# A two-layer graph-attention kernel: VectorE's second inputs moved to PSUM, the last denominators summed on TensorE, LayerNorms in the value bank, the mask built in pieces

## The chip, the cores and the metric

The kernel runs on one core of one Trainium2 chip. The metric is the time of one execution on the device in microseconds (us). The engines are called by the names that the profile uses: PE is TensorE, PEld its weight loads, DVE is VectorE, ACT is ScalarE, POOL is GpSimd and SP is SyncE, which issues most transfers.

## The reference, cut to what matters

```python
def _gat_layer(h, mask, b):                       # N = 2048 nodes, D = 64
    scores = jnp.einsum('...nd,...md->...nm', h, h)
    scores = jnp.where(mask, scores, -1e16)
    attn = jax.nn.softmax(scores, axis=-1)
    return jnp.einsum('...nm,...md->...nd', attn, h) + b

mask = graph + eye(N) > 0
h    = einsum('bnc,hdc->bhnd', x, Wh)             # B = 8 batches, H = 4 heads
cat  = _gat_layer(h, mask, bh) -> [B, N, H*D]     # first layer
h2   = einsum('bnk,dk->bnd', leaky_relu(cat, 0.2), Wo)
z2   = leaky_relu(_gat_layer(h2, mask, bo), 0.2)  # second layer
out  = layernorm(z2) * gamma + beta
return layernorm(x + out)
```

Everything is fp32. The score matrices dominate: 2048 x 2048 for each of 32 pairs of batch and head, and for 8 batches in the second layer.

## The kernel before

The work is cut into 20 units. A unit is two heads (first layer, 16 units) or two batches (second layer, 4 units), stacked as 2 x 64 rows. A unit has four chunks of 512 query columns, a chunk has four periods, and a period has four blocks of 128 keys. In a period TensorE computes the scores of four blocks and then the values of the four blocks before them:

```python
def scores(self, c, m):
    ps = spsum(...)                        # 3 PSUM tiles of two banks
    for j in range(2):
        nc.tensor.matmul(ps[:, j*W:(j+1)*W], self.hT[rows, m*P:(m+1)*P], self.hT[rows, c*W:(c+1)*W], ...)
    e = slot([P, 2, W], F32, ...)
    nc.vector.tensor_tensor(e, ps, mask[c][:, m, :], OP.subtract)      # L523
    nc.scalar.activation(e, e, AF.Exp, bias=shift, scale=1.0)          # L525
    return e

def values(self, c, m, e):                 # O[c] is one PSUM bank, one buffer
    for j in range(2):
        nc.tensor.matmul(self.O[c][j*D:(j+1)*D, :], self.hN[:, m, j*D:(j+1)*D], e[:, j, :], ...)
```

The softmax denominators are sums of `e` over all 16 blocks and 128 partitions. GpSimd adds 12 of the 16 tiles (11 additions), VectorE the fourth tile of each period (L549, L553) and the two partial sums (L560); TensorE sums the result over the partitions with a matrix of ones. The rest is spread over the following periods, one step in each:

```python
def finish0(self, c):                      # one period after the last values
    nc.scalar.copy(self.osb[c], self.O[c])
    nc.vector.tensor_tensor(self.acc[c], self.acc[c], self.accd[c][0], OP.add)     # L560
def finish1(self, c):
    for j in range(2):
        nc.tensor.matmul(pz[j*D:(j+1)*D, :], ones, self.acc[c][:, j, :], ...)      # 64-column tiles
    nc.scalar.copy(zsb, pz)
    ... two small transfers spread one row of zsb over the partitions: zt
def finish2(self, c):
    nc.vector.reciprocal(rt, self.zt)
    nc.vector.tensor_tensor(stat[:, 0, :], stat[:, 0, :], self.zt, OP.add)         # L579
    nc.vector.tensor_tensor(stat[:, 1, :], stat[:, 1, :], rt, OP.add)
    ... rt to DRAM (rd) and back, broadcast over 64 partitions: rz
def finish3(self, c):
    nc.vector.tensor_tensor(z, z, self.rz[c], OP.mult)                             # L589
    nc.vector.scalar_tensor_tensor(z, z, SLOPE, z, OP.mult, OP.max)                # L590
def finish4(self, c): ...   # projection by Wo (first layer); turn and first LayerNorm (second)
def finish5(self, c): ...   # gamma, beta, + x, second LayerNorm, store (second layer)
```

Both LayerNorms work on a tile `y` in SBUF. `at(t, job)` puts a job behind the scores, values and additions of period `t`. The mask is built during the first unit from rows of the adjacency matrix, half a row block at a time.

Of the kernel before, what the change touches and what calls it, by code (L numbers as in the profile page):

```python
# [33 lines left out]
EPS = 1e-5  # L35
# [317 lines left out]
def fast_kernel(ctx: ExitStack, tc: tile.TileContext, x, adj, Wh, bh, Wo, bo, gamma, beta, out, flag):  # L353
# [11 lines left out]
    K = 2 * CB  # L365

    const = ctx.enter_context(tc.tile_pool(name="const", bufs=1))
    big = ctx.enter_context(tc.tile_pool(name="big", bufs=2))
    epool = ctx.enter_context(tc.tile_pool(name="epool", bufs=12))
    accs = ctx.enter_context(tc.tile_pool(name="accs", bufs=2))  # L370
    work = ctx.enter_context(tc.tile_pool(name="work", bufs=6))
# [11 lines left out]
    def tpsum(name):  # L383
        return psum.tile([P, W], F32, tag="t", name=name, bufs=1)
# [9 lines left out]
    ones = const.tile([P, D], F32, name="ones")  # L394
    nc.gpsimd.memset(ones, 1.0)
    shifts = const.tile([P, 3], F32, name="shifts")
    nc.gpsimd.memset(shifts[:, 0:1], -SHIFT1)
    nc.gpsimd.memset(shifts[:, 1:2], -SHIFT2)
    nc.gpsimd.memset(shifts[:, 2:3], BIG)
    mhalf = const.tile([P, K], F32, name="mhalf")  # L400
# [7 lines left out]
    stat = const.tile([P, 2, 8], F32, name="stat")  # L408
    nc.gpsimd.memset(stat, 0.0)
# [37 lines left out]
    def load_adj(r, h):  # L447
        st = slot([P, N // 2], I32, f"adj{r}_{h}")
        nc.sync.dma_start(out=st, in_=adj[r * P:(r + 1) * P, h * N // 2:(h + 1) * N // 2])
        return st  # L450

    def build_mask(r, h, st):
        if r // (NB // 2) == h:
            c0 = r * P - h * N // 2
            nc.vector.tensor_tensor(st[:, c0:c0 + P], st[:, c0:c0 + P], ident, OP.add)
        m = slot([P, N // 2], BF16, f"mrow{r}_{h}")
        if h == 0:
            nc.scalar.activation(m, st, AF.Relu, bias=shifts[:, 2:3], scale=-BIG)
        else:
            nc.vector.tensor_scalar(m, st, 0.0, BIG, OP.is_le, OP.mult)  # L460
        p = spsum(f"pm{r}_{h}", BF16)
        for k in range(NB // 2):
            nc.tensor.transpose(p[:, k * P:(k + 1) * P], m[:, k * P:(k + 1) * P], identb)  # L463
        c, i0 = divmod(r * P, W)
        dst = mask[c][:, h * NB // 2:(h + 1) * NB // 2, i0:i0 + P]
        src = p[:, :NB // 2 * P].rearrange("p (m i) -> p m i", i=P)
        if h == 0:
            nc.vector.tensor_copy(dst, src)
        else:
            nc.scalar.copy(dst, src)  # L470

    pw = tpsum("pw")
# [8 lines left out]
    class Unit:  # L481


        def __init__(self, n, bp, b2, hp):
            self.n, self.bp, self.b2, self.hp = n, bp, b2, hp
            self.second = hp is None
            self.osb, self.rz, self.acc, self.accd, self.O = {}, {}, {}, {}, {}
# [40 lines left out]
        def values(self, c, m, e):  # L528
            if m == 0:
                self.O[c] = psum.tile([P, W], F32, tag="o", name=f"o{self.n}_{c}", bufs=1)  # L530
            for j in range(2):
                nc.tensor.matmul(self.O[c][j * D:(j + 1) * D, :], self.hN[:, m, j * D:(j + 1) * D], e[:, j, :],  # L532
                                 start=(m == 0), stop=(m == NB - 1))

        def add_up(self, c, es):

            first = c not in self.acc
            if first:
                self.acc[c] = accs.tile([P, 2, W], F32, tag="acc", name=f"acc{self.n}_{c}")
                self.accd[c] = [es[3]]  # L540
                nc.gpsimd.tensor_tensor(self.acc[c], es[0], es[1], OP.add)  # L541
                nc.gpsimd.tensor_tensor(self.acc[c], self.acc[c], es[2], OP.add)  # L542
                return
            for e in es[:3]:
                nc.gpsimd.tensor_tensor(self.acc[c], self.acc[c], e, OP.add)  # L545
            if len(self.accd[c]) == 1:
                held = self.accd[c][0]
                t = accs.tile([P, 2, W], F32, tag="accd", name=f"accd{self.n}_{c}", bufs=1)
                nc.vector.tensor_tensor(t, held, es[3], OP.add)  # L549
                self.accd[c] = [t, 2]  # L550
            else:
                t = self.accd[c][0]
                nc.vector.tensor_tensor(t, t, es[3], OP.add)  # L553
                self.accd[c][1] += 1


        def finish0(self, c):
            self.osb[c] = wtile(f"osb{self.n}_{c}")
            nc.scalar.copy(self.osb[c], self.O[c])
            nc.vector.tensor_tensor(self.acc[c], self.acc[c], self.accd[c][0], OP.add)  # L560

        def finish1(self, c):
            n = self.n
            pz = tpsum(f"pz{n}_{c}")
            for j in range(2):
                nc.tensor.matmul(pz[j * D:(j + 1) * D, :], ones, self.acc[c][:, j, :], start=True, stop=True)  # L566
            zsb = wtile(f"zsb{n}_{c}")
            nc.scalar.copy(zsb, pz)
            self.zt = small.tile([P, 8], F32, tag="zt", name=f"zt{n}_{c}")
            with nc.allow_non_contiguous_dma(reason="2 KB"):  # L570
                for j in range(2):
                    nc.sync.dma_start(out=self.zt[j * D:(j + 1) * D, :],
                                      in_=zsb[j * D:j * D + 1, :].rearrange("o (p k) -> o p k", k=8))

        def finish2(self, c):
            n = self.n
            rt = small.tile([P, 8], F32, tag="rt", name=f"rt{n}_{c}")
            nc.vector.reciprocal(rt, self.zt)
            nc.vector.tensor_tensor(stat[:, 0, :], stat[:, 0, :], self.zt, OP.add)  # L579
            nc.vector.tensor_tensor(stat[:, 1, :], stat[:, 1, :], rt, OP.add)  # L580
            rd = dram.tile([2, W], F32, tag="rd", name=f"rd{n}_{c}")
            nc.sync.dma_start(out=rd.rearrange("j (p k) -> (j p) k", k=8), in_=rt)
            self.rz[c] = wtile(f"rz{n}_{c}")
            for j in range(2):
                nc.sync.dma_start(out=self.rz[c][j * D:(j + 1) * D, :], in_=rd[j].partition_broadcast(D))

        def finish3(self, c):
            z = self.osb[c]
            nc.vector.tensor_tensor(z, z, self.rz[c], OP.mult)  # L589
            nc.vector.scalar_tensor_tensor(z, z, SLOPE, z, OP.mult, OP.max)  # L590

        def finish4(self, c):
            n, z = self.n, self.osb[c]
            p = tpsum(f"pp{n}_{c}")
# [11 lines left out]
            for i in range(CB):  # L606
                nc.tensor.transpose(p[:, i * P:(i + 1) * P], z[:, i * P:(i + 1) * P], ident)
            rows = p.rearrange("p (k d) -> p k d", d=D)
            self.y = wtile(f"y{n}_{c}")
            self.norm(c, rows, 0)  # L610

        def finish5(self, c):
            if not self.second:
                return
            y = self.y.rearrange("p (k d) -> p k d", d=D)
            nc.vector.tensor_mul(y, y, gam.unsqueeze(1).to_broadcast([P, K, D]))
            nc.vector.tensor_add(y, y, bet.unsqueeze(1).to_broadcast([P, K, D]))
# [5 lines left out]
            nc.vector.tensor_add(self.y, self.y, xr)  # L623
            self.norm(c, y, 1)
            yv = self.y.rearrange("p (i b d) -> p i b d", b=2, d=D)
# [3 lines left out]

        def norm(self, c, src, tag):  # L630
            n = self.n
            y = self.y.rearrange("p (k d) -> p k d", d=D)
            st = small.tile([P, 4, K], F32, tag="st", name=f"st{n}_{c}_{tag}")
            sq = wtile(f"sq{n}_{c}_{tag}").rearrange("p (k d) -> p k d", d=D)
            nc.vector.tensor_reduce(st[:, 0, :], src, AX.X, OP.add)
            nc.vector.tensor_scalar(st[:, 0, :], st[:, 0, :], 1.0 / D, None, OP.mult)
            nc.vector.tensor_tensor(y, src, st[:, 0, :].unsqueeze(2).to_broadcast([P, K, D]), OP.subtract)  # L637
            nc.scalar.square(sq, y)  # L638
            nc.vector.tensor_reduce(st[:, 1, :], sq, AX.X, OP.add)
            nc.vector.tensor_scalar(st[:, 2, :], st[:, 1, :], 1.0 / D, EPS, OP.mult, OP.add)  # L640
            nc.gpsimd.tensor_tensor(st[:, 3, :], st[:, 2, :], mhalf, OP.pow)  # L641
            nc.vector.tensor_mul(y, y, st[:, 3, :].unsqueeze(2).to_broadcast([P, K, D]))  # L642
# [21 lines left out]
    transpose_x(0, x0, 0)  # L664
    transpose_x(0, x0, 1)
    raw = {}
    halves = [(r, h) for r in range(NB) for h in range(2)]
    AHEAD = 3
    for k in range(2 * CB):
        raw[k] = load_adj(*halves[k])  # L670
        if k >= AHEAD:
            build_mask(*halves[k - AHEAD], raw.pop(k - AHEAD))
    for part in range(4):
        units[0].prepare(part)
    for k in range(2 * CB, len(halves) + AHEAD):
        t = (k - 2 * CB) // 2

        def job(k=k):
            if k < len(halves):
                raw[k] = load_adj(*halves[k])  # L680
            build_mask(*halves[k - AHEAD], raw.pop(k - AHEAD))
# [97 lines left out]
```

## Time and profile before

The time is 3559.51 us (median of three runs, 3554.14 to 3559.91).

| | before |
|---|---|
| granted TensorE clock, mean | 0.910 |
| busy: TensorE, VectorE, ScalarE, GpSimd | 81%, 83%, 47%, 67% |
| one TensorE period, undisturbed | 7.22 us |
| a first-layer unit (four chunks) after the first | 153 to 159 us; 168 just after a second-layer unit |
| a second-layer unit | 212 to 216 us |
| first scores; end of the first unit's first chunk | 46.8 us; 119.9 us |

A unit's length is read between the first finishing operations of successive units (the accumulation L560 before, the maximum L583 after). In a line of groups the columns are: line, engine, operation, output and inputs by the program's names, shapes, count, then busy us in total and mean ns of one, then the engine's idle time just ahead of them and what ended it. In a timeline they are start, length in us, engine, line, operation, count, and in brackets the idle time before it with its releaser. Four undisturbed periods and the small TensorE work of a chunk would make about 32 us, so a first-layer chunk (38 to 40 us) loses 6 to 8 us and a second-layer chunk (54 us) over 20.

### The profile page before, as it was taken

How to read it: one execution, taken by the hardware profiler on the slowest of the kernel's cores; microseconds unless marked ns; L12 is line 12 of the kernel's file. 1: busy time of each engine (PE TensorE's matmuls, PEld its weight loads, DVE VectorE, ACT ScalarE, POOL GpSimd, SP SyncE). 2: the span in 40 equal slices, each digit the busy share in tenths (PEclk: the TensorE clock that was granted, in tenths of full speed). 3: DMA queues.
4: the chain of work that ended last, by engine and by line, in shares of the span. 5: the costliest groups of instructions: out<-in, count | busy, mean ns of one | idle time of the engine just before them, and what ended most of it. 6: DMA issues, size and time to landing. Idle time of an engine off the chain costs nothing.

```text
span 3551.6 us, 31313 instructions
## 1 busy us (share of the span) xinstructions
PE 2870.1 (81%) x11526; PEld 986.6 (28%) x11526; DVE 2963.9 (83%) x2368; ACT 1654.9 (47%) x1577; POOL 2363.0 (67%) x929
## 2 busy tenths in 40 slices
PE   5668888988876788898887688888889888877663
PEld 3232323332222232232222222323323232222221
DVE  4668888889888888888888888898888889888886
ACT  3435555554543445555444345555545555443332
POOL 2437777777755677777775577777777777766553
PEclk8779999999988899999998899999999999988886
DMA  3210000000000000000000000000000000000000
GB/s 118 63 33 7 10 7 7 19 10 7 7 16 13 12 10 7 19 7 10 7 10 18 10 10 10 6 19 6 10 7 7 7 10 6 7 10 18 12 15 22
DMA packets 93125, 53.57 MB, mean 15 GB/s; under 512 B 78466, under 2 KB 78530, under 8 KB 92962
## 3 DMA queue, kind: packets, MB, share of 16 engines
q1 hardware_dynamic: 92162, 51.02, 5.1%
q8 instruction: 92, 1.51, 0.2%
q0 software_dynamic: 176, 0.26, 0.1%
q14 instruction: 71, 0.58, 0.1%
q10 hardware_dynamic: 624, 0.20, 0.0%
HBM read 46.60 MB, written 4.52 MB: 14 GB/s over the span
## 4 chain that ended last, share of the span: by engine, by line
PE 38%; DVE 29%; issue 19%; POOL 8%; DMA 4%; ACT 2%; SPq 0%; DVEq 0%; POOLq 0%; ACTq 0%
PE o L532 17%; PE s L520 15%; DVE e L523 11%; POOL acc L545 5%; DVE osb L589 5%; DVE accd L553 4%; DMA rz<-rd 4%; DVE acc L560 3%; PE ph L501 2%; PE pz L566 2%; POOL acc L542 1%; DVE y L642 1%; POOL acc L541 1%; ACT e L525 1%; PE pp L599 1%
## 5 line engine op out<-in xcount | busy, mean ns | idle before, releaser
L545 POOL TENSOR_TENSOR acc<-acc,e 128x1024 f32<-128x1024 f32 x720 | 1869.8, 2597 | 467.2 <-ACT e L525 421.1
L525 ACT ACTIVATE e<-e,shifts 128x1024 f32<-128x1024 f32 x1280 | 1451.0, 1149 | 1355.6 <-DVE e L523 1348.3
L523 DVE TENSOR_TENSOR e<-s,mask 128x1024 f32<-128x1024 f32 x1280 | 1477.6, 1212 | 278.5 <-PE s L520 266.6
L520 PE MATMUL s<-hT 64*128 64x512 f32 x4096 | 1096.5, 646 | 340.5 <-DVE e L523 284.5
L532 PE MATMUL o<-e,hN 128*64 128x512 f32 x5120 | 1285.2, 648 | 0.0
L520 PEld LDWEIGHTS s<-hT 64*128 64x128 f32 x4096 | 393.1, 195 | 944.8 <-DVE e L523 459.4
L532 PEld LDWEIGHTS o<-e,hN 128*64 128x64 f32 x5120 | 367.1, 149 | 933.8 <-issue 712.5
L520 PE MATMUL s<-h2T 64*128 64x512 f32 x1024 | 286.8, 679 | 196.1 <-DVE e L523 166.1
L541 POOL TENSOR_TENSOR acc<-e,e 128x1024 f32<-128x1024 f32 x80 | 188.9, 2362 | 345.6 <-ACT e L525 345.6
L553 DVE TENSOR_TENSOR accd<-accd,e 128x1024 f32<-128x1024 f32 x160 | 310.4, 1940 | 0.0
L641 POOL TENSOR_TENSOR st<-st,mhalf 128x8 f32<-128x8 f32 x32 | 52.7, 1647 | 358.9 <-DVE st L640 358.9
L542 POOL TENSOR_TENSOR acc<-acc,e 128x1024 f32<-128x1024 f32 x80 | 248.6, 3107 | 6.3
L589 DVE TENSOR_TENSOR osb<-osb,rz 128x512 f32<-128x512 f32 x80 | 220.1, 2751 | 4.9 <-DMA rz<-rd 4.9
L590 DVE SCALAR_TENSOR_TENSOR osb<-osb 128x512 f32<-128x512 f32 x80 | 210.8, 2635 | 2.8
L520 PEld LDWEIGHTS s<-h2T 64*128 64x128 f32 x1024 | 97.4, 200 | 350.9 <-DVE e L523 215.7
L560 DVE TENSOR_TENSOR acc<-acc,accd 128x1024 f32<-128x1024 f32 x80 | 169.4, 2118 | 2.8
L579 DVE TENSOR_TENSOR stat<-stat,zt 128x8 f32<-128x8 f32 x80 | 169.3, 2116 | 0.0
L642 DVE TENSOR_TENSOR y<-y,st 128x512 f32<-128x512 f32 x32 | 81.8, 2555 | 56.3 <-POOL st L641 56.3
L549 DVE TENSOR_TENSOR accd<-e,e 128x1024 f32<-128x1024 f32 x80 | 121.1, 1514 | 0.0
L463 PE MATMUL pm<-identb,mrow 128*128 128x128 bf16 x256 | 29.5, 286 | 87.0 <-DVE mrow L460 49.1
L566 PE MATMUL pz<-acc,ones 128*64 128x512 f32 x320 | 85.0, 611 | 9.5 <-DVE acc L560 9.5
L638 ACT ACTIVATE sq<-y 128x512 f32<-128x512 f32 x32 | 20.1, 629 | 142.8 <-DVE y L637 142.8
(70 smaller groups left out, 811.1 us busy)
## 6 DMA issues: line engine op xcount, KB each, us to landing
rz<-rd SPq DMA_DIRECT2D x160, 128.0 KB, 2.8
adj<-in_adj_dram SPq DMA_DIRECT2D x32, 512.0 KB, 3.7
x<-in_x_dram SPq DMA_DIRECT2D x16, 256.0 KB, 3.7
xr<-in_x_dram SPq DMA_DIRECT2D x32, 128.0 KB, 2.6
out_dram<-y SPq DMA_DIRECT2D x32, 128.0 KB, 2.0
zt<-zsb SPq DMA_DIRECT2D x160, 2.0 KB, 1.7
rd<-rt SPq DMA_DIRECT2D x80, 4.0 KB, 1.4
ws<-in_L_gnn_Wh_dram ACTq DMA_DIRECT2D x2, 64.0 KB, 4.7
```

The costliest lines, as they stand in the source:

```text
L520: nc.tensor.matmul(ps[:, j * W:(j + 1) * W], self.hT[rows, m * P:(m + 1) * P], self.hT[rows, c * W:(c + 1) * W], start=True, stop=True)
L523: nc.vector.tensor_tensor(e, ps.rearrange("p (j i) -> p j i", j=2), mask[c][:, m, :].unsqueeze(1).to_broadcast([P, 2, W]), OP.subtract)
L525: nc.scalar.activation(e, e, AF.Exp, bias=shifts[:, 1:2] if self.second else shifts[:, 0:1], scale=1.0)
L532: nc.tensor.matmul(self.O[c][j * D:(j + 1) * D, :], self.hN[:, m, j * D:(j + 1) * D], e[:, j, :], start=(m == 0), stop=(m == NB - 1))
L541: nc.gpsimd.tensor_tensor(self.acc[c], es[0], es[1], OP.add)
L542: nc.gpsimd.tensor_tensor(self.acc[c], self.acc[c], es[2], OP.add)
L545: nc.gpsimd.tensor_tensor(self.acc[c], self.acc[c], e, OP.add)
L553: nc.vector.tensor_tensor(t, t, es[3], OP.add)
L560: nc.vector.tensor_tensor(self.acc[c], self.acc[c], self.accd[c][0], OP.add)
L579: nc.vector.tensor_tensor(stat[:, 0, :], stat[:, 0, :], self.zt, OP.add)
L589: nc.vector.tensor_tensor(z, z, self.rz[c], OP.mult)
L590: nc.vector.scalar_tensor_tensor(z, z, SLOPE, z, OP.mult, OP.max)
```

## The change

Its intent is to take VectorE off the critical path. Where VectorE had two inputs in SBUF, one is now in PSUM. The last three blocks' denominators, which come too late for GpSimd, go straight to TensorE in 32-column tiles. The LayerNorms stay in the PSUM bank of the values, and the matrix that turns the tile also takes out the mean. The mask comes in pieces that each finish two key blocks of one query chunk. The core of the diff:

```diff
+    DIRECT = 3
-    epool = ... bufs=12        # slots for e
+    epool = ... bufs=14
+    def opsum(name):           # two value banks instead of one and one "t" bank
+        return psum.tile([P, W], F32, tag="o", name=name, bufs=2)
...
-        def add_up(self, c, es): ... three tiles to GpSimd, the fourth to VectorE
+        def add_up(self, c, m, e):
+            elif m < NB - DIRECT:
+                nc.gpsimd.tensor_tensor(acc, acc, e, OP.add)
+            else:
+                self.terms[c].append(e)
...
+        def sums(self, c):
+            for k in range(half):
+                for s in range(2):
+                    for j in range(2):
+                        q = (2 * s + j) * 32
+                        nc.tensor.matmul(pz[q:q + 32, :W], ones, terms[s * half + k][:, j, :],
+                                         start=(k == 0), stop=(k == half - 1), tile_position=(0, q))
+            nc.scalar.copy(zsb, pz[:, :W])
+            ... four small transfers instead of two: zt
+            nc.scalar.mul(o5, self.O[c], SLOPE)
+            nc.vector.tensor_tensor(self.O[c], self.O[c], o5, OP.max)
+        def invert(self, c):
+            nc.vector.tensor_reduce(zall[:, k, :], zt, AX.X, OP.add)
+            nc.vector.reciprocal(rt, zall[:, k, :])
+            ... rt to DRAM and back
+        def scale(self, c):
+            nc.vector.tensor_tensor(self.z[c], self.O[c], self.z[c], OP.mult)
...
-                nc.tensor.transpose(p[:, i * P:(i + 1) * P], z[:, i * P:(i + 1) * P], ident)
+                nc.tensor.matmul(p[:, i * P:(i + 1) * P], z[:, i * P:(i + 1) * P], centre, ...)
+        def norm1(self, c, y):  # y is the PSUM bank
+            nc.vector.tensor_mul(y, y, self.rstd(c, y, 0))   # square, reduce, ScalarE, power on GpSimd
+            nc.vector.tensor_mul(y, y, gam...)
+            nc.vector.tensor_add(y, y, bet...)
+            nc.vector.tensor_add(y, y, xr)
+        def norm2(self, c): ... mean, power, product, store
...
+                at((t + 1, "mid"), lambda u=u, c=c: u.sums(c))      # between scores and values
+                at(t + 1, lambda u=u, c=c: u.invert(c))             # after the values
+                at(t + 2, lambda u=u, c=c: u.scale(c))
+                at(t + 3, lambda u=u, c=c: u.project(c))            # holds norm1
+                at(t + 4, lambda u=u, c=c: u.norm2(c))
```

## The prediction

> **What bounds the kernel now.** I read the page first (busy shares, chain, groups), then the timeline of single chunks, then durations of single lines, then the table by stage.
>
> ```profile
> PE 2870.1 (81%) x11526; PEld 986.6 (28%) x11526; DVE 2963.9 (83%) x2368; ACT 1654.9 (47%) x1577; POOL 2363.0 (67%) x929
> PE 38%; DVE 29%; issue 19%; POOL 8%; DMA 4%; ACT 2%; SPq 0%; DVEq 0%; POOLq 0%; ACTq 0%
> L545 POOL TENSOR_TENSOR acc<-acc,e 128x1024 f32<-128x1024 f32 x720 | 1869.8, 2597 | 467.2 <-ACT e L525 421.1
> L523 DVE TENSOR_TENSOR e<-s,mask 128x1024 f32<-128x1024 f32 x1280 | 1477.6, 1212 | 278.5 <-PE s L520 266.6
> L553 DVE TENSOR_TENSOR accd<-accd,e 128x1024 f32<-128x1024 f32 x160 | 310.4, 1940 | 0.0
> L589 DVE TENSOR_TENSOR osb<-osb,rz 128x512 f32<-128x512 f32 x80 | 220.1, 2751 | 4.9 <-DMA rz<-rd 4.9
> L590 DVE SCALAR_TENSOR_TENSOR osb<-osb 128x512 f32<-128x512 f32 x80 | 210.8, 2635 | 2.8
> L560 DVE TENSOR_TENSOR acc<-acc,accd 128x1024 f32<-128x1024 f32 x80 | 169.4, 2118 | 2.8
> L579 DVE TENSOR_TENSOR stat<-stat,zt 128x8 f32<-128x8 f32 x80 | 169.3, 2116 | 0.0
> ```
>
> No engine is full; the chain alternates between TensorE and VectorE. A 128x8 addition (L579) takes 2116 ns: that is waiting, not work. The durations (minimum/median/maximum) of two lines say how much:
>
> ```profile
> L590 DVE SCALAR_TENSOR_TENSOR osb<-osb x80: 691/2711/2717, 173.6 to 3526.7; 128x512 f32<-128x512 f32 x80
> L545 POOL TENSOR_TENSOR acc<-acc,e x720: 2337/2381/3249, 62.0 to 3498.9; 128x1024 f32<-128x1024 f32 x180
> ```
>
> 691 ns is the operation, the other 2.0 us most of a GpSimd addition. The timeline shows one undisturbed period (four blocks of scores, four of values) of a first-layer unit, then the place in a second-layer unit where VectorE is late:
>
> ```profile
> 626.80 3.70 PE L520 MATMUL s<-hT 64*128 64x512 f32 x16
> 630.43 3.65 PE L532 MATMUL o<-e,hN 128*64 128x512 f32 x16
> 634.02 2.85 PE L520 MATMUL s<-hT 64*128 64x512 f32 x12
> ...
> 1124.69 2.82 DVE L642 TENSOR_TENSOR y<-y,st 128x512 f32<-128x512 f32 x1 [1.76 <-POOL st L641]
> 1127.43 3.35 DVE L560 TENSOR_TENSOR acc<-acc,accd 128x1024 f32<-128x1024 f32 x1
> 1131.98 2.08 PE L520 MATMUL s<-hT 64*128 64x512 f32 x4 [9.58 <-DVE e L523]
> 1133.99 5.61 PE L532 MATMUL o<-e,hN 128*64 128x512 f32 x16
> ```
>
> The period has a TensorE pitch of 634.02 - 626.80 = 7.22 us. TensorE runs only three score tiles ahead of VectorE, so every lump of VectorE work beyond some 2.6 us stops it: here 9.58 us, after which the same matmuls ran slower (2.08 us for 4, elsewhere 1.13). By stage (length, busy times, granted clock): start and mask, a first-layer unit, a second-layer unit with its neighbours.
>
> ```profile
> 0.00:300.00 300.00, 200.52 (x854) 88.07 (x856) 181.51 (x152) 119.95 (x113) 118.03 (x61) 0.83 0.20 64
> 592.00:749.00 157.00, 139.35 (x580) 48.48 (x576) 137.87 (x105) 82.38 (x79) 115.55 (x44) 0.96 0.06 14
> 1870.00:2083.00 213.00, 155.76 (x566) 50.99 (x562) 177.62 (x157) 81.72 (x80) 126.85 (x51) 0.84 0.06 14
> ```
>
> Spacing the values' matmuls through the trace, a first-layer chunk (four periods) takes 8.2 + 11.8 + 10.1 + 8.1 = 38.2 us, 39.3 with the preparation (157 / 4); a second-layer chunk 12.3 + 20.6 + 13.5 + 8.1 = 54.5 us. There are 64 and 16 of them.
>
> **What the Trainium skill says.** "SBUF — State Buffer", Who interferes with whom: VectorE with two SBUF inputs contends with a GpSimd instruction that reads SBUF, with at most one it does not. The trace agrees (691 against 2711 ns above; L523, one input from PSUM, stays at 1212). "VectorE: DVE Perf Modes", The perf-mode tier table: fp32 tensor_tensor runs at the base rate from SBUF and PSUM alike, so the move costs no rate; the trace has 686 ns for h2T<-h2T,pp (512 columns, one input from PSUM). "TensorEngine Tiling (Array Packing)", Tiling Modes: with 128 rows, 32-column tiles give four tiles at once, and changing the mode drains the array. The trace shows only two at once: 16 value records of 512 columns in some 3.6 us. "TensorE: Matmul & The Clock Gate", Part 1: an idle array has its clock lowered; the 0.84 of the second-layer stage against 0.96 agrees.
>
> **The change part by part.** Durations of rows not shown (L549, L580, the LayerNorm lines, ph, pn) are from the same view of groups.
> VectorE loses L553 310, L549 121, L560 169, L589 220, L590 211, L579 and L580 182: 1213 us. It gains, per chunk, a maximum in PSUM and a scaling at 0.69 each and a reduction of some 0.17: 80 x 1.55 = 124. LayerNorms: nine operations of 0.69 on 16 chunks, about 100 instead of some 165; mask: 32 copies of 0.69 = 22 instead of 62. Estimated VectorE busy time: 2964 - 1213 + 124 - 65 - 40 = 1770 us, 22 us of a chunk. It stops being a bound.
> GpSimd gets 12 additions per chunk instead of 11, at the undisturbed 2.4 us: 960 x 2.4 = 2304, + 53 for the powers = 2360 us, 29.5 us a chunk, below TensorE.
> ScalarE: the slope copy replaces the eviction of O; unchanged, 1660 us.
> TensorE: the denominators become eight matmuls of 512 columns in groups of four at once, two rounds of 0.86 + about 0.2 for switching = 1.9 us instead of 1.0. TensorE per first-layer chunk: 4 x 7.22 = 28.9, + 1.9, + projection 1.0, + preparation 1.5 (the next unit's projection ph, 32 x 1.7, its transposes pn, 40 x 1.05, and those of x, over 80 chunks) = 33.3 us.
> A wait takes its place. The denominators' inversion now stands in the same period as their sum; VectorE waits in order for their transfer. From the period's start: last exponential at 6.9, zsb copied at 7.5, four issues of 0.55, landing 1.7 to 1.85: 11.1 us; with reduction, reciprocal and the next e, 12.7. TensorE starts the next period at 3.6 + 1.9 + 3.6 = 9.1 and wants that tile at 9.1 + 2.6 = 11.7. About 1.1 us lost per chunk: 34.4 us. The rd/rz round trip (5.1 us at the end of the trace) ends at 16.6, just before the next period needs VectorE.
> Second layer: norm1 starts after the projection (8.2 us), then square 0.65, reduction 0.7, ScalarE 0.3, GpSimd 1.65, four times 0.7: VectorE free at 14.6, the next e at 15.8, wanted at 10.8: 5.0 lost. norm2 has the same loop but starts before the period ends: 3.4 lost. Inversion 1.5. Sum 28.9 + 1.9 + 1.0 + 9.9 = 41.7; the slower clock after such gaps cost up to 2.9 us before (5.61 - 3.65 + 2.08 - 1.13), I take 3.3 for both: 45 us.
> Start: the first scores needed eight mask halves and came at 46.8 us; now they need two turned pieces, about 28. The mask then takes 15 periods of 9.1 instead of some 15 to 17, plus waits of ScalarE on GpSimd for the diagonal of perhaps 12 us: first unit 4 x 34.4 + 15 x 1.85 + 12 = 178 us. The end, after the last values, was 54 us; its links now add to about 42.
> Sum: 28 + 178 + 60 x 34.4 + 16 x 45 + 42 = 28 + 178 + 2064 + 720 + 42 = 3032. Against 3559 the gains are 60 x 4.9 = 294, 16 x 9.5 = 152, and about 80 at start and end.
>
> **The rivals.**
> TensorE bound without the new waits: 28.9 + 1.9 + 1.0 + 1.5 on all chunks and no LayerNorm stall, about 2750 us. For it: the 1.00 clock of the quoted period. Against: VectorE is in order, and the LayerNorm loops over ScalarE and GpSimd remain.
> The new wait is bigger: if the four small transfers or rz come 2 us later than I count, each chunk loses 2 to 4 us, 160 to 320: 3200 to 3350. For it: SyncE issues in order, with the mask's loads in the same queue. Against: zt lands in 1.7 us throughout.
> GpSimd becomes the bound: 29.5 us of 34.4, and it lags by up to some 7 us within a chunk; with 14 slots a score tile may wait for its slot, or a power queue behind additions. Worth perhaps 60 to 100 us. Against: nothing contends any more, and on average it catches up.
> The four-tile matmuls run two at a time: + 1.7 x 80 = 137 us. Nothing in this trace decides it.
>
> **Range and chances.** The TensorE part (about 2670 us of the sum) is measured here; the waits, some 300 us, are argued. A miss of a third of them is 100 us each way. Predicted 3030 us, range 2920 to 3140. Faster by over 2% 0.97, within 2% 0.02, slower 0.01: only a wrong sign of several terms could eat 500 us.
>
> **What would show it right or wrong.** Right: no VectorE group with median above 1.3 us; GpSimd additions at about 2.4 us, 960 of them; VectorE about 50 to 60% busy, TensorE above 88%; first-layer chunks of 33 to 36 us; the reduction of zt waiting for its transfer; second-layer chunks of 42 to 48 with a wait on GpSimd's power. Wrong: the pz group at 3 us or more a chunk, TensorE's waits on e longer than 1.5 us in first-layer chunks, e or exponentials waiting for GpSimd, or a granted clock below 0.9 in the first layer.

## The result, and the profile after

The kernel after takes 2929.29 us (median of four runs, 2927.95 to 2929.53); the kernel before took 3557.11 us in the same rounds. Ratios here are the mean time of one kernel's runs over that of the other's of the same rounds, so they are not quite the ratio of the medians quoted. This one is 0.8234, with a 95% interval from 0.822 to 0.8249. The granted clock rose from 0.910 to 0.977. The predicted 3030 us were 101 us too high, and the range holds the result near its lower end.

The page of the kernel after, its busy line, its chain and three of its groups:

```profile
PE 2730.6 (93%) x12550; PEld 967.9 (33%) x12550; DVE 1799.2 (61%) x1861; ACT 1656.4 (57%) x1625; POOL 2331.8 (80%) x1025
PE 60%; ACT 14%; DVE 11%; DMA 5%; issue 4%; SPq 3%; POOL 2%; ACTq 0%; DVEq 0%; POOLq 0%
L554 POOL TENSOR_TENSOR acc<-acc,e 128x1024 f32<-128x1024 f32 x880 | 2079.9, 2363 | 79.5 <-ACT e L534 13.0
L583 DVE TENSOR_TENSOR o<-o,o 128x512 f32<-128x512 f32 x80 | 56.0, 700 | 175.8 <-ACT o L582 175.8
L599 DVE TENSOR_TENSOR z<-o,z 128x512 f32<-128x512 f32 x80 | 55.2, 690 | 53.5 <-DMA z<-rd 53.4
```

VectorE lost 1165 us of busy time and has fallen behind TensorE and GpSimd. Its share of the chain fell from 29% to 11%, TensorE's rose from 38% to 60%. What the prediction put down to GpSimd's reads is gone: the maximum (L583) and the scaling (L599) take 0.70 and 0.69 us where their forerunners took 2.64 and 2.75, and no VectorE group has a mean above 1.23 us. A GpSimd addition takes 2363 ns in the mean, 2597 before. The idle times of L583 and L599, and of the reduction of zt below, are the new waits.

What matters is TensorE's own wait for a score tile. The view of waits (engine, line, what it waited for, us in total, times, longest), first of the kernel before, then of the kernel after:

```profile
PE s L520 <- DVE e L523: 450.6, 203, 9.6
```

```profile
DVE zall L589 <- DMA zt<-zsb: 199.0, 78, 4.2
PE s L529 <- DVE e L532: 116.4, 86, 4.8
```

TensorE's wait shrank from 450.6 to 116.4 us. VectorE's 199.0 us of waiting for a transfer is larger, but costs only as much of it as reaches TensorE. The table by stage has the length, then the busy time of each engine, then the clock: the start, a first-layer unit, a second-layer unit.

```profile
0.00:300.00 300.00, 278.20 (x1412) 110.47 (x1414) 179.75 (x191) 187.99 (x179) 220.04 (x122) 0.99 0.23 67
501.70:639.10 137.40, 134.84 (x626) 48.41 (x624) 85.67 (x87) 80.54 (x76) 113.44 (x49) 1.00 0.03 9
772.00:944.70 172.70, 147.00 (x636) 51.51 (x634) 106.84 (x119) 86.09 (x95) 123.68 (x56) 0.92 0.08 19
```

Against the three lines that the prediction shows, TensorE's busy time in the start rises from 200.5 to 278.2 of 300 us, the first-layer unit is 98% TensorE (134.84 of 137.40), and only the second-layer unit still has a clock below 0.99. Lengths by stage:

| | before | predicted | after |
|---|---|---|---|
| first scores | 46.8 us | 28 | 29.2 |
| first scores to the 16th period's end | | 178 | 153.0 |
| first-layer chunk, preparation shared out | 38 to 40 | 34.4 | 33.9 (mean of 15 units, 135.6 / 4) |
| second-layer chunk, same | 53 to 54 | 45 | 42.8 (mean of 3 units, 171.1 / 4) |
| after the last values | 54 | 42 | 45 |

Two timelines show the two kinds of chunk. First the period in which a first-layer chunk's denominators are summed and inverted:

```profile
602.48 1.46 PE L569 MATMUL pz<-e,ones 128*32 128x512 f32 x10
603.87 3.65 PE L541 MATMUL o<-e,hN 128*64 128x512 f32 x16
607.46 2.85 PE L529 MATMUL s<-hT 64*128 64x512 f32 x12
609.51 0.17 DVE L589 TENSOR_REDUCE zall<-zt 128x8 f32<-128x16 f32 x1 [2.50 <-DMA zt<-zsb]
611.08 1.13 PE L529 MATMUL s<-hT 64*128 64x512 f32 x4 [0.78 <-DVE e L532]
...
615.72 3.71 PE L529 MATMUL s<-hT 64*128 64x512 f32 x16
```

The denominators' 16 records (10 of them in the first line; the first of all is at 602.02) are done when the values start at 603.87, after 1.85 us. The reduction is released 11.2 us after the period's scores began (598.27, not shown), VectorE comes late to the next score tile, and TensorE stands for 0.78 us. The next period's scores start 615.72 - 607.46 = 8.26 us after this one's, against 7.22 undisturbed: the short stop costs 1.04 us, more than the idle time that the view shows. Then the first LayerNorm of a second-layer chunk:

```profile
880.13 1.65 POOL L628 TENSOR_TENSOR st<-st,mhalf 128x8 f32<-128x8 f32 x1 [1.31 <-ACT st L627]
881.81 0.70 DVE L637 TENSOR_TENSOR o<-o,st 128x512 f32<-128x512 f32 x1 [2.10 <-POOL st L628]
...
885.89 2.08 PE L529 MATMUL s<-hT 64*128 64x512 f32 x4 [4.75 <-DVE e L532]
887.89 5.61 PE L541 MATMUL o<-e,hN 128*64 128x512 f32 x16
...
896.63 1.13 PE L529 MATMUL s<-hT 64*128 64x512 f32 x4 [0.35 <-DVE e L532]
```

VectorE waits for the power on GpSimd, makes its four products and sums, and TensorE has stood for 4.75 us by then. The scores and values that follow run slowly (2.08 for 1.13 us, 5.61 for 3.65). The second LayerNorm, one period later, costs TensorE only 0.35 us.

### The profile page after: what moved, and what is told of

It is laid out like the page before. It is cut to its first block, busy times and chain, and to the rows that moved or that the text cites. A ratio compares the mean times of both kernels' runs of the same rounds, so it can differ in the third digit from the quotient of the medians.

```text
span 2927.8 us, 33405 instructions
## 1 busy us (share of the span) xinstructions
PE 2730.6 (93%) x12550; PEld 967.9 (33%) x12550; DVE 1799.2 (61%) x1861; ACT 1656.4 (57%) x1625; POOL 2331.8 (80%) x1025
## 4 chain that ended last, share of the span: by engine, by line
PE 60%; ACT 14%; DVE 11%; DMA 5%; issue 4%; SPq 3%; POOL 2%; ACTq 0%; DVEq 0%; POOLq 0%
PE o L541 28%; PE s L529 25%; ACT e L534 11%; DVE e L532 6%; DMA zt<-zsb 4%; SPq L578 3%; PE ph L510 2%; PE o L608 2%; POOL st L628 2%; ACT zsb L572 1%; PE pn L520 1%; ACT o L582 1%; PE pz L569 1%; DVE hN L522 1%; DVE st L626 1%
## 5 line engine op out<-in xcount | busy, mean ns | idle before, releaser
L554 POOL TENSOR_TENSOR acc<-acc,e 128x1024 f32<-128x1024 f32 x880 | 2079.9, 2363 | 79.5 <-ACT e L534 13.0
L532 DVE TENSOR_TENSOR e<-s,mask 128x1024 f32<-128x1024 f32 x1280 | 1475.6, 1215 | 348.2 <-PE s L529 333.0
L541 PE MATMUL o<-e,hN 128*64 128x512 f32 x5120 | 1188.4, 607 | 0.0
L529 PE MATMUL s<-hT 64*128 64x512 f32 x4096 | 1004.3, 609 | 65.7 <-DVE e L532 65.7
L583 DVE TENSOR_TENSOR o<-o,o 128x512 f32<-128x512 f32 x80 | 56.0, 700 | 175.8 <-ACT o L582 175.8
L569 PE MATMUL pz<-e,ones 128*32 128x512 f32 x960 | 154.1, 601 | 0.0
L589 DVE TENSOR_REDUCE zall<-zt 128x8 f32<-128x16 f32 x80 | 13.7, 171 | 199.1 <-DMA zt<-zsb 199.0
L569 PE MATMUL pz<-acc,ones 128*32 128x512 f32 x320 | 84.7, 600 | 6.2 <-POOL acc L554 2.2
L599 DVE TENSOR_TENSOR z<-o,z 128x512 f32<-128x512 f32 x80 | 55.2, 690 | 53.5 <-DMA z<-rd 53.4
L522 DVE TENSOR_TENSOR hN<-pn,bhb 128x1024 f32<-128x1024 f32 x32 | 39.1, 1223 | 51.8 <-PE pn L520 51.8
L510 PE MATMUL ph<-xT,whT 64*128 64x512 f32 x128 | 66.6, 644 | 0.0
L608 PE MATMUL o<-z,woT 128*64 128x512 f32 x128 | 65.5, 593 | 0.0
```

The costliest lines, as they stand in the source:

```text
L510: nc.tensor.matmul(p[:, q * W:(q + 1) * W], whT[rows, self.hp * P:(self.hp + 1) * P], xT[self.bp][rows, (2 * h + q) * W:(2 * h + q + 1) * ...
L522: nc.vector.tensor_add(self.hN[:, h * NB // 2:(h + 1) * NB // 2, :], p.rearrange("p (m d) -> p m d", d=P), b.unsqueeze(1).to_broadcast([P, ...
L529: nc.tensor.matmul(ps[:, j * W:(j + 1) * W], self.hT[rows, m * P:(m + 1) * P], self.hT[rows, c * W:(c + 1) * W], start=True, stop=True)
L532: nc.vector.tensor_tensor(e, ps.rearrange("p (j i) -> p j i", j=2), mask[c][:, m, :].unsqueeze(1).to_broadcast([P, 2, W]), OP.subtract)
L541: nc.tensor.matmul(self.O[c][j * D:(j + 1) * D, :], self.hN[:, m, j * D:(j + 1) * D], e[:, j, :], start=(m == 0), stop=(m == NB - 1))
L554: nc.gpsimd.tensor_tensor(acc, acc, e, OP.add)
```

## The experiments

All are timed in three rounds beside the kernel before (3558 to 3561 us); "after" stands for 2929.29 us. All gave correct results. In the texts A is my theory in each, B and C are the rivals that the text names. My theory throughout: TensorE's pitch sets the pace, and anything on another engine costs only as far as it makes a score tile late for TensorE.

**late_invert: half a period's room for the transfer.** The inversion and the scaling move between scores and values of the following period.

```diff
-                at(t + 1, lambda u=u, c=c: u.invert(c))
-                at(t + 2, lambda u=u, c=c: u.scale(c))
+                at((t + 2, "mid"), lambda u=u, c=c: u.invert(c))
+                at((t + 3, "mid"), lambda u=u, c=c: u.scale(c))
```

> The inversion is issued after the scores of the next period, the scaling after those of the one after it; nothing else moves. Theory A (in order VectorE waits about 2.5 us for the transfer of zt, and TensorE loses 0.75 us by it in every first-layer chunk, 0.7 to 1.7 in a second-layer one): the wait for zt goes from 199 us to near 0 and the time falls by 50 to 80 us, to 2850 to 2880. Theory B (the loss is only where the pipeline shows its slack, and something else stops TensorE there if it doesn't): unchanged within 10 us.

Measured 2863.02 us (2862.22 to 2863.69), ratio 0.8044, 66 us below after. The wait for zt fell from 199.0 to 4.2 us, TensorE's wait for VectorE from 116.4 to this:

```profile
PE s L529 <- DVE e L532: 66.3, 22, 5.5
```

A bare first-layer chunk (one that prepares nothing for the next unit) fell from 32.7 to 31.7 us: its third period takes 7.22 us again instead of 8.26. That the new wait was real is shown; 66 us over 80 chunks are 0.8 us each, less than 1.04 because in the chunk that prepares the next unit the wait costs nothing (its third period takes 8.93 us in both runs). The new wait was the placing of the inversion, not the transfer itself.

**direct5: GpSimd relieved.** TensorE sums five blocks instead of three, GpSimd makes 10 additions instead of 12.

```diff
-    DIRECT = 3
+    DIRECT = 5
```

> TensorE sums the last five blocks instead of three: one more round of four 32-column matmuls, 0.86 us of TensorE in each chunk, 69 us in all, and two GpSimd additions fewer (10, 24 us a chunk). Theory A: the longer period gives the zt transfer 0.86 us more, so the 0.75 us stall of TensorE goes and the time stays within 15 us of 2929. Theory B (TensorE time simply adds): 2998. Theory C (GpSimd's backlog costs time now): it falls by 30 us or more.

Measured 2944.55 us, ratio 0.827, 15 us above after. GpSimd's busy time fell from 2332 to 1955 us and nothing was won, so GpSimd did not bound the kernel. TensorE's busy time rose by 63 us; the time rose by less because TensorE's waits for VectorE shrank from 116.4 to 67.9 us. TensorE's added work was taken partly out of its waits: in a bare first-layer chunk the period with the denominators grew from 9.19 to 10.05 us and the next one fell from 8.26 to 7.41.

**pz_two_tiles: 32-column tiles against 64-column ones.** The denominators are summed with halves (0.5, so the two equal rows add up to one denominator) in the two 64-column tiles that the values use; otherwise all is the same.

```diff
-            for k in range(half):
-                for s in range(2):
-                    for j in range(2):
-                        q = (2 * s + j) * 32
-                        nc.tensor.matmul(pz[q:q + 32, :W], ones, terms[s * half + k][:, j, :], ...,
-                                         tile_position=(0, q))
+            for k in range(len(terms)):
+                for j in range(2):
+                    nc.tensor.matmul(pz[j * D:(j + 1) * D, :W], halves64, terms[k][:, j, :], ...)
```

> The denominators by 64-column tiles, two at once, four rounds: the group takes 3.5 us instead of 1.85. Theory A: 1.7 us more of TensorE a chunk, less the 0.75 us stall that it hides: + 0.95 x 80 = 76, some 3005 us. If TensorE time simply adds: + 136, 3065. If the 32-column tiles did not run four at a time, no change.

Measured 2987.44 us, ratio 0.8392, 58 us above after. In its timeline the 16 records start at 615.20 and the values at 618.65: 3.45 us instead of 1.85. The four narrow tiles do run four at a time. Of the 1.6 us x 80 = 128 us of added work some 70 were again taken out of the stop at the inversion: the period after the denominators takes 7.2 to 7.6 us in most bare first-layer chunks instead of 8.26.

**sbuf_inputs: the contention put back.** ScalarE copies the values to SBUF, and the maximum and the scaling take both inputs from SBUF, as before the change.

```diff
+            self.osb[c] = wtile(f"osb{n}_{c}")
+            nc.scalar.copy(self.osb[c], self.O[c])
-            nc.vector.tensor_tensor(self.O[c], self.O[c], o5, OP.max)
+            nc.vector.tensor_tensor(self.osb[c], self.osb[c], o5, OP.max)
...
-            nc.vector.tensor_tensor(self.z[c], self.O[c], self.z[c], OP.mult)
+            nc.vector.tensor_tensor(self.z[c], self.osb[c], self.z[c], OP.mult)
```

> ScalarE copies O to SBUF again, and the maximum and the scaling take two SBUF inputs; numbers of VectorE instructions unchanged. Theory A (TensorE sets the pace, VectorE's waits on GpSimd cost only what exceeds its slack): both take 2.7 us instead of 0.7, VectorE busy rises by some 320 us, but the maximum ends before zt lands, and the scaling delays the next tile by some 0.4 us: + 20 to 70 us, 2950 to 3000. Theory B (the waits[...] were what the old kernel lost): + 250 to 320 us, 3180 to 3250.

Measured 2956.53 us, ratio 0.8306, 27 us above after. The group of the scaling in this run:

```profile
L602 DVE TENSOR_TENSOR z<-osb,z 128x512 f32<-128x512 f32 x80 | 133.5, 1669 | 53.8 <-DMA z<-rd 53.7
```

It takes 1669 ns in the mean (690 after), the maximum 1592 (700). VectorE's busy time rose by 147 us, and the time by 27: most of the contention falls into VectorE's slack. The wait for zt fell from 199 to 89 us at the same time, for the longer maximum fills it. The run has 80 more copies on ScalarE too, so not all of the 27 us need be contention.

**before_direct: the denominators alone, on the kernel before.** GpSimd makes 12 additions, TensorE sums the last three blocks in 32-column tiles, and VectorE makes no addition; everything else is the kernel before.

```diff
+            elif m < NB - DIRECT:
+                nc.gpsimd.tensor_tensor(acc, acc, e, OP.add)
             else:
-                t = self.accd[c][0]
-                nc.vector.tensor_tensor(t, t, es[3], OP.add)
+                self.acc[c].append(e)
...
-            nc.vector.tensor_tensor(self.acc[c], self.acc[c], self.accd[c][0], OP.add)
```

> The kernel before with this one part of the change: GpSimd adds blocks 0 to 12, TensorE sums the last three and the accumulator with 32-column tiles; no addition of denominators on VectorE; masks, LayerNorms, slope and scaling as before. Theory A (the old kernel lost where VectorE came late to the next score tile, and these additions were the largest part of that): first-layer chunks of 35 to 36.5 us instead of 38.2 to 39.3, second-layer ones of 47 to 50 instead of 54.5: 3180 to 3280 us, about half of the gain. Theory B (the lumps of slope, scaling and LayerNorm dominate anyway): above 3400.

Measured 3109.53 us (3107.44 to 3114.01), ratio 0.8736: 451 us below before (3560.06), 72% of the whole gain and more than I expected. Its page:

```profile
PE 2767.3 (89%) x12486; PEld 965.2 (31%) x12486; DVE 2216.9 (71%) x2128; ACT 1656.6 (53%) x1577; POOL 2361.8 (76%) x1010
```

VectorE lost 747 us of busy time, more than the 600 us of the three lines taken out (L549, L553, L560), since the small additions to `stat`, the multiplication and the slope also wait less. The multiplication and the slope still have two SBUF inputs and take 1834 and 2340 ns in the mean; in the first-layer chunk that I read in the timeline they stop TensorE for 1.42 us:

```profile
1139.43 1.13 PE L523 MATMUL s<-hT 64*128 64x512 f32 x4 [1.42 <-DVE e L526]
```

That period takes 9.8 us, and 10.1 in most bare first-layer chunks: 2.9 more than an undisturbed one, of which about 0.9 is the projection. Bare first-layer chunks took 33.6 us and a unit 34.4 in the mean of its chunks, below the 35 to 36.5 expected; most second-layer chunks took 46.6 to 49.4, about as expected. So the two operations that were left, contention included, cost about 2 us in a chunk where nothing hides them, and my expectation had charged them too high.

**old_mask: only the mask undone.** The kernel after with the mask of before, which needs eight half rows ahead of the first scores instead of pieces (diff: the two mask functions and their schedule as before).

```diff
-    def load_adj(c, g): ...      # 4 query blocks x 2 key blocks
-    def mask_rows(c, g, st): ... # ScalarE, diagonal on GpSimd
-    def mask_turn(c, g, m): ...
+    def load_adj(r, h): ...      # 1 query block x 8 key blocks
+    def build_mask(r, h, st): ...
```

> The changed kernel with the mask built by half rows as before (eight halves before the first scores, comparison and diagonal on VectorE too). Only the start and the first unit can change: if the mask by pieces is worth what the two traces differ by in that stretch beyond the four or five chunks' own gain, + 70 to 100 us, 3000 to 3030; if VectorE's relief alone made the first unit faster, + 20 to 40.

Measured 3006.39 us, ratio 0.8445, 77 us above after. The second unit's first maximum comes at 305.1 us instead of 230.2, which is 75 us; from there on the units have the same lengths. The mask's pieces are worth 77 us, 75 of them before the second unit's first maximum.

**ln_in_sbuf: the LayerNorms put back into SBUF.** ScalarE copies the turned rows to SBUF, and both norms work there.

```diff
-            self.norm1(c, p.rearrange("p (k d) -> p k d", d=D))
+            self.ysb = wtile(f"y{self.n}_{c}")
+            nc.scalar.copy(self.ysb, p)
+            self.norm1(c, self.ysb.rearrange("p (k d) -> p k d", d=D))
```

> The changed kernel with the LayerNorms in SBUF: ScalarE copies the projected rows out of PSUM, and the norms' sums and products take two SBUF inputs. Theory A (the first product after each power collides with the GpSimd addition that starts at the same moment): the two products by the power take 2.8 us instead of 0.7, the others stay at 0.7; 4 to 5 us a second-layer chunk, + 60 to 100 us, 2990 to 3030. Theory B (TensorE's slower clock hides it as it hid the second norm): + 20 or less.

Measured 3009.68 us, ratio 0.8451, 80 us above after. Its timeline at the first product, after the power:

```profile
897.63 2.82 DVE L639 TENSOR_TENSOR y<-y,st 128x512 f32<-128x512 f32 x1 [2.09 <-POOL st L630]
...
903.82 2.08 PE L529 MATMUL s<-hT 64*128 64x512 f32 x4 [7.51 <-DVE e L532]
```

The product takes 2.82 us (0.70 in PSUM), because the power that releases it also releases GpSimd's next addition. The stall grows from 4.75 to 7.51 us and a second-layer chunk from 41.6 to 47.0 us. Of the stall's 2.76 us the product is 2.12 and the new copy ahead of the square about 0.6. So most of the 80 us is the same kind of contention that cost at most 27 us over 80 chunks above: here it lies in the one chain that TensorE waits for.

**adds_on_vector: the additions put back on VectorE.** VectorE adds blocks 3, 7 and 11 from SBUF, GpSimd makes 10 additions, and TensorE sums the two partial sums and the last two blocks. There are 13 slots for `e` instead of 14.

```diff
-    DIRECT = 3
+    DIRECT = 2
+            elif m == 7:
+                nc.vector.tensor_tensor(accd, self.terms[c][1], e, OP.add)
+            elif m == 11:
+                nc.vector.tensor_tensor(self.terms[c][1], self.terms[c][1], e, OP.add)
```

> The changed kernel with two of the additions of each chunk on VectorE from SBUF (blocks 3, 7 and 11), ten on GpSimd, and the same four terms for TensorE; 13 slots for score tiles instead of 14, to make room. Theory A (only what exceeds VectorE's slack of some 2.6 us in a period counts): VectorE busy + 250 to 350 us, time + 50 to 130: 2980 to 3060. Theory B (VectorE's busy time counts): + 250 or more.

Measured 2927.37 us, ratio 0.8223: no change. The second of VectorE's additions in this run:

```profile
L559 DVE TENSOR_TENSOR accd<-accd,e 128x1024 f32<-128x1024 f32 x80 | 169.4, 2118 | 0.0
```

VectorE's busy time rose by 271 us to 2070.5, and all of it is hidden; TensorE waited 117.7 us for VectorE, as after. Both theories had expected a loss, so both missed here, mine by less. In this kernel nothing is gained by taking these additions off VectorE. (GpSimd has 377 us less in direct5 and wins nothing, so its two additions fewer are not what paid for them here.)

**ln_split: the LayerNorm chain spread over periods.** Square, reduction and power stay in the projection's period; the products come between scores and values of the next; the second power and the last product go to GpSimd one period later. The addition of beta, to x instead of to the norm, goes to GpSimd as well.

```diff
-            nc.vector.tensor_mul(y, y, self.rstd(c, y, 0))
+            self.r1 = self.rstd(c, sq, 0)
...
+                at((t + 4, "mid"), lambda u=u, c=c: u.norm1b(c))     # products, + x, mean
                 at(t + 4, lambda u=u, c=c: u.norm2(c))              # less the mean, square
+                at((t + 5, "mid"), lambda u=u, c=c: u.norm2b(c))     # power and product on GpSimd, store
```

> The changed kernel with each LayerNorm cut where it leaves VectorE: square, sum and power in one place, the four products and sums after the scores of the next period, the second norm's mean into SBUF, its power and last product on GpSimd after the scores of the period after that. Theory A (in order VectorE stands 4.5 us in each norm for ScalarE and GpSimd, and TensorE loses 4.75 us plus 2.9 us of slower clock by it per chunk): second-layer chunks of 34 to 35.5 us instead of 41.6, 2929 - 115 = 2815 (2790 to 2840). Theory B (the work moved into the other periods stops TensorE there): 2880 or more.

Measured 2911.32 us, ratio 0.8175: 18 us below after instead of the 115 that I expected. The timeline shows where the rest went:

```profile
1558.04 0.93 SPq L672 DMA_DIRECT2D out_dram<-xr  x2
...
1562.67 0.17 DVE L589 TENSOR_REDUCE zall<-zt 128x8 f32<-128x16 f32 x1 [5.80 <-DMA zt<-zsb]
...
1564.22 2.08 PE L529 MATMUL s<-h2T 64*128 64x512 f32 x4 [4.32 <-DVE e L532]
```

SyncE issues in order. The store of the output, which waits for GpSimd's product, now stands ahead of the next chunk's zt, issued at 1559.06, so the inversion comes late and TensorE stands for 4.32 us. The LayerNorm's stall was removed and a transfer's wait took its place; the chunks stayed at 41.1 us.

**both: ln_split and late_invert together.** (The two diffs above.)

> Late inversion and cut LayerNorms together. If the two losses are separate: 2863 - 115 = 2750 (2725 to 2775). If they share slack, less than the sum: above 2790.

Measured 2847.11 us, ratio 0.7996, 16 us below late_invert; I had expected 2725 to 2775. The wait for zt is gone (4.1 us in all), but VectorE now waits 74.1 us in 13 chunks for the first power on GpSimd, which had waited 33.5 us in 16 chunks after. The power stands behind a backlog of additions in GpSimd's order.

**both_relief: two additions fewer on GpSimd in the second layer.**

```diff
-            elif m < NB - DIRECT:
+            elif m < NB - (DIRECT + 2 if self.second else DIRECT):
```

> As the run with late inversion and cut LayerNorms, but in second-layer units TensorE sums the last five blocks, so that GpSimd has 10 additions there instead of 12. In that run VectorE waited 74 us for the power on GpSimd, which stood behind a backlog of additions. Theory A (GpSimd's backlog took the place of the wait removed): second-layer chunks fall from 41.0 to 34.5 to 36 us, the wait for the power to under 20 us, 2847 - 16 x 5.5 = 2760 (2740 to 2800). Theory B (VectorE's moved lump alone stops TensorE): 2840 to 2865, the added TensorE round included.

Measured 2825.49 us, ratio 0.7937, between the theories. The wait for the power is still 44.4 us in 11 chunks. Three lines of one such chunk:

```profile
1519.20 21.93 POOL L554 TENSOR_TENSOR acc<-acc,e 128x1024 f32<-128x1024 f32 x9
1541.08 1.65 POOL L626 TENSOR_TENSOR st<-st,mhalf 128x8 f32<-128x8 f32 x1
...
1547.86 2.08 PE L529 MATMUL s<-hT 64*128 64x512 f32 x4 [5.52 <-DVE e L532]
```

GpSimd runs nine additions without a gap and the power only then, 7 us after its input was ready (1534.0, from the timeline). The chunk's additions had started late: the previous chunk's second power (at 1514.05) and product stood ahead of the first of them in GpSimd's order.

**ordered: the second norm's end after the additions.** One word differs from both_relief: the job stands behind the period's additions instead of ahead of them.

```diff
-                at((t + 5, "mid"), lambda u=u, c=c: u.norm2b(c))
+                at(t + 5, lambda u=u, c=c: u.norm2b(c))
```

> As the run before (late inversion, cut LayerNorms, ten GpSimd additions in second-layer units), with one move: the second norm's end (its sum, power, last product and store) is issued after the additions of its period and after the transfers of zt, not before them. In the run before, GpSimd started a chunk's ten additions only after that power and product, at 1516.8, though their tiles were ready from about 1509; they ended at 1541, and the next chunk's power, wanted at 1534, stood behind them, so VectorE waited 4.57 us and TensorE 5.52 us. Theory A (the order in GpSimd's queue makes the loss): additions end some 5 us earlier, VectorE's wait for the power falls from 44 us to under 15, second-layer chunks from 40 to about 35 us: 2825 - 16 x 4.5 = 2750 (2735 to 2785). Theory B (VectorE's lump of four products is what stops TensorE): 2805 or more.

Measured 2770.15 us (2768.27 to 2771.27), ratio 0.7777 (0.7764 to 0.779), 159 us below after and the fastest version. Its page, and its timeline at the first norm of a second-layer chunk:

```profile
PE 2692.9 (97%) x12678; PEld 968.6 (35%) x12678; DVE 1769.2 (64%) x1829; ACT 1657.6 (60%) x1625; POOL 2293.3 (83%) x1025
```

```profile
1448.71 1.65 POOL L626 TENSOR_TENSOR st<-st,mhalf 128x8 f32<-128x8 f32 x1 [5.40 <-ACT st L625]
...
1457.84 1.13 PE L529 MATMUL s<-h2T 64*128 64x512 f32 x4 [0.86 <-DVE e L532]
```

The power starts at once, GpSimd having been idle for 5.40 us. TensorE's wait for VectorE is 13.9 us in the whole run (116.4 after), most second-layer chunks take 34 to 36.5 us, the clock is 0.991, and TensorE is busy for 97% of the span. This is what late_invert and ln_split were worth, with two GpSimd additions fewer in the second layer, once neither's gain was eaten by an order of issue; whether the new order would have done without the fewer additions no run shows.

## Why the prediction was right, and where it was off

**The mechanism was right.** The prediction said that the kernel is TensorE's pitch plus what other engines add by coming late, and each such term was seen: the denominators in 1.85 us (1.9 predicted), the inversion waiting for its transfer at 11.2 us (11.1), and the first LayerNorm's stall of 4.75 us (5.0; the terms printed for it add up to 14.3, not 14.6). VectorE's busy time was 1799 us (1770, partly by luck: the old LayerNorm lines add up to about 192 us, not 165), GpSimd's 2332 (2360), ScalarE's 1656 (1660), a GpSimd addition 2.36 us (2.4).

**Second layer, the largest miss: 16 x (45 - 42.8) = 35 us.** The failing step is "norm2 has the same loop but starts before the period ends: 3.4 lost", and the 3.3 us for the clock added on top. The stall at norm2 measured 0.35 us. After norm1's stall TensorE's scores and values ran 2.9 us longer, and in that time VectorE caught up. The two losses overlap, and I added them. The trace tests this: in the nine second-layer chunks without preparation the period with norm1's stall takes 13.88 to 15.20 us (the clock is low for 3.4 us in one of them and for 6.8 in the others) and the next 11.10 to 9.80, and their sum is 24.99 to 25.00 us in every one. What the slow clock takes in the first comes back in the second; VectorE's chain sets the sum. Against 7.22 + 9.19 undisturbed the two norms and the clock cost 8.6 us together, not 5.0 + 3.4 + 3.3 = 11.7. A chunk is then 28.9 + 2.0 (denominators) + 1.1 (projection) + 8.6 + 1.1 (inversion) = 41.7, as seen without preparation. The 45 had left out the preparation, 1.2 us in the mean, so the miss looks smaller than it was, by luck.

**First layer: 60 x (34.4 - 33.9) = 30 us.** The pitch was right, and so was the wait for the inversion in a bare chunk (1.04 us, 1.1 predicted); in the mean of a unit late_invert gave back 0.9, since the preparation hides some of it. The rest is the projection, 0.85 us instead of 1.0 (a period of 8.07), and the preparation, 1.3 instead of 1.5 (late_invert: 33.0 in the mean, 31.7 bare).

**The start: 24 us.** "The mask then takes 15 periods of 9.1 ... plus waits of ScalarE on GpSimd for the diagonal of perhaps 12 us": the first unit's periods took 8.1 to 11.5 us, one with the mask alone 8.68 instead of 9.1, and the 16 came to 153.0 us from the first scores instead of 178 (the first scores came 1.2 us late). That is less than the predicted sum without its 12 us, so the waits for the diagonal did not add up as an extra. That the mask is worth 77 us is shown by old_mask, against my "about 80 at start and end".

**The end: 3 us the other way** (45 for 42). Together 35 + 30 + 24 - 3 = 86 of the 101 us. The other 15 I put down to where the stages are cut (a chunk's finishing work runs in the next chunk's periods, the last one's in the end); that is not shown.

**The rivals.** "TensorE bound without the new waits", about 2750 us, was not this kernel; ordered came within 20 us of it, to 2770, by removing the waits that I had held against it. "The new wait is bigger" is refuted by late_invert (66 us). "GpSimd becomes the bound" is refuted for this kernel by direct5; yet its detail, "a power queue behind additions", came true in both, where it cost most of the expected gain. "The four-tile matmuls run two at a time" is refuted by the 1.85 us and by pz_two_tiles.

**Where the gain came from.** The denominators alone gave 451 us on the kernel before. Undone one by one in the kernel after, the mask is worth 77, the LayerNorms in PSUM 80, the PSUM input of the slope and scaling 27. The sum of these three, 184, happens to fit 628 - 451 = 177. But the parts are not independent: adds_on_vector shows the additions back on VectorE costing nothing once the rest is done. It leaves GpSimd 10 additions and spares VectorE the last sum (L560), so it does not undo the denominators in full; no run here does that. As I read these runs, the change brought VectorE's work between score tiles below TensorE's pitch: four subtractions take 4.6 of a period's 7.22 us, which leaves VectorE some 2.6. Within that, 271 us more were free; a longer lump stops TensorE (9.58 us at one place before). Two parts of the diff no run undoes alone: the second value bank and the two more slots. In the kernel before, the values' matmuls (L532) show 0.0 us of idle time, so nothing there points to the bank.

## What to carry to other kernels

Find the engine that sets the pace and ask of each piece of other work only whether it makes that engine's next input late; 271 us of VectorE work cost nothing here, and two products made 2.1 us longer in one chain cost most of 80. Two losses that follow each other are not to be added before asking whether the first gives the second its time back; a constant sum of two varying periods shows that it does. When a chain is spread over engines that run in order, the place in each engine's order (here SyncE's store and GpSimd's power) decides whether the gain arrives: one job moved behind the additions was worth 55 us.

## What the Trainium skill lacked or had wrong

- "TensorE: Matmul & The Clock Gate", Part 1, lowers the clock after at least one idle window of some 3.4 us. The low-clock stretches here do last one, two or three times 3.41 us, but a shorter gap can bring one: in direct5 a gap of 2.10 us (856.45 to 858.55) was followed by a clock of 0.50 from 860.16 to 863.57, while in the kernel before a gap of 3.25 us (3423.42 to 3426.67) was not.
- The same part has the array back at full clock around 4 us into sustained activity. After the gap of 4.75 us shown above the clock was 0.50 until 891.88, for 6.0 us of work, and 2.9 us were lost. (The page's window runs freely, so it leaves room for this.)
- "TensorEngine Tiling (Array Packing)", Tiling Modes, gives 128 x 32 as four tiles but no fp32 time for it. Here 16 fp32 records of 512 columns took 1.85 us in four 32-column tiles and 3.45 us in two 64-column tiles, from the first of them to the next matmul: a factor of 1.86.
- No page gives the time of a power on GpSimd. Here a 128 x 8 power took 1.65 us, more than two VectorE operations on 128 x 512 and a third of the first LayerNorm's stall.
